# Two moves in the order of a transformer's layer slots: a norm's second parts behind the divisions, a residual between two steps of Q's rotation

## The chip, the cores and the metric

The kernel runs on one core of one Trainium2 chip. The metric is device time in microseconds (us) of one execution. The core has five engines that run beside each other and wait for one another through semaphores: TensorE (PE; its weight loads are listed apart as PEld), VectorE (DVE), ScalarE (ACT), GpSimd (POOL) and SyncE (SP), which issues the transfers. TensorE writes to PSUM, of which there are eight banks.

## The reference

Four sequences of 512 tokens with 128 channels pass through one attention of 16 heads and then through six layers. All is in float32. A layer is a local attention and a gated feed-forward step (FFN), each with a token shift ahead of it and a residual behind it:

```python
def attn_layer(x, Wqkv, qs, ksc, Wo):
    q, k, v = jnp.split(x @ Wqkv, 3, -1)      # 16 heads of 64
    q = l2norm(q) * qs
    k = l2norm(k) * ksc
    q = q * cos * scale + rotate_half(q) * sin * scale
    k = k * cos * inv + rotate_half(k) * sin * inv
    out = local_attention(q, k, v)            # windows of 32, each with the one before it
    return out @ Wo

def ffn_layer(x, g, bln, W1, b1, W2, b2):
    mu = x.mean(-1, keepdims=True)
    var = ((x - mu) ** 2).mean(-1, keepdims=True)
    xn = (x - mu) / jnp.sqrt(var + 1e-05) * g + bln
    a, gate = jnp.split(xn @ W1 + b1, 2, -1)
    return a * jax.nn.gelu(gate, approximate=False) @ W2 + b2

for i in range(DEPTH):                        # 6
    x = attn_layer(shift_tokens(x), ...) + x
    x = ffn_layer(shift_tokens(x), ...) + x
```

## The kernel before

The first 569 us or so hold the attention ahead of the layers, which the change does not touch. The layers are worked as a pipeline of 96 units: layer by layer, sequence by sequence, tile by tile of 128 tokens (four tiles, T = 0 to 3, to a sequence). A loop calls `slot(n, ...)` for n = -1 to 94, and each slot works on several units at once:

- unit n (`u`): its scores, softmax and product with V;
- unit n-1 (`prev`): its output projection and residual;
- unit n+1 (`nxt`): the transposes of its Q and K;
- unit n+2 (`new`): the projections of its Q, K and V, and the rotation of Q and K.

Between them stand, by a plan, the steps of the FFN of the sequence before. For a sequence whose FFN begins in the slot n of a first tile (T = 0), the shift of its tokens (`move`) stands in slot n, the norm's mean, variance and scale (`norm`) in slots n+1 to n+3, so in T = 1 to 3, and the FFN's chunks and its output (`geglu`) in slots n+3 to n+6. Each of the three norm steps has a second part: a Square on ScalarE (L104) behind the mean; the reciprocal root behind the variance (two VectorE steps, L81 and L82, and twelve GpSimd steps, L84 to L87); and one VectorE step with the norm's gain and bias (L123, tile hT) behind the scale. A second part is not issued at once but put into the list `later`.

The order of the work is written out by hand: each engine works its instructions in the order in which the kernel's scheduled program holds them. The lines that matter here, with the engine of each:

- L659 and L670 (PE): scores; L680 and L682 (DVE): their maximum and its subtraction; L688 (ACT): exponents.
- `project`, L521 (PE): a projection of 1024 columns in two halves of 512, into two PSUM banks. `square`, L533 (ACT), and `sum_squares`, L538 (DVE), give the norms of the heads.
- `rotate`, L543 and L549 (DVE): the two products of the rotation, both read from PSUM; between them it can issue other steps (`between`). `add_rotated`, L560 (POOL), adds the two. `over_norm`, L568 (POOL), divides by the norms; ahead of it come L564, L81 and L82 (DVE) and L84 to L87 (POOL).
- `transposed`, L632 (PE) and L635 (ACT): four transposes into one bank, and the copy out of it; for P (tile pr, copy pT), Q, K and the output. Two banks (`one_t`) serve these, the output projection and the norms.
- `times_v`, L702 (PE), in two groups; L711 and L712 (DVE): the division of each.
- `project_out_2`, L727 (PE), and `residual`, L735 (DVE), which reads the projection's bank.
- FFN: shift L153 to L155 (POOL); chunk L771 and L772 (PE), L775 (ACT), L779 (DVE); output L791 (PE), L794 (DVE).

In the slot of a first tile (`first`) the kernel before projects one half of K, rotates Q and issues the residual ahead of the transposes of P; the other half of K stands between the two groups of these transposes. In the other slots the residual comes first, K's first half stands between the transposes and its other half behind them, with Q's rotation. In all slots the list `later` is issued between the two products of K's rotation.

Of the kernel before, what the change touches and what calls it, by code (L numbers as in the profile page):

```python
# [32 lines left out]
def body(ctx: ExitStack, tc: tile.TileContext, a, out: bass.AP):  # L33
# [37 lines left out]
    def new_xT():  # L71
        return res.tile([P, S], F32, tag="xT", name="xT", bufs=B + 2)
# [102 lines left out]
    with tc.manual_schedule():  # L175
# [105 lines left out]
        class Rows:  # L281
# [5 lines left out]
            def scores(self):  # L287
                b, c, t = self.b, self.c, self.t
                sc = self.sc = ps1.tile([P, 2, S], F32, tag="sc", name="ps_sc", bufs=2)
                for k0 in range(0, S, S // 2):  # L290
                    for h in range(2):
                        rows = slice(h * HD, (h + 1) * HD)
                        mm(
                            sc[:, h, k0 : k0 + S // 2],
                            lhsT=qs[b, c][rows, t * P : (t + 1) * P],
                            rhs=ks[b, c][rows, k0 : k0 + S // 2],
                            start=(k0 == 0),
                            stop=False,
                            skip_group_check=True,
                        )  # L300
# [173 lines left out]
    def load_part(i, j):  # L474

        w = wts.tile([P, INNER], F32, tag=f"wqkv{j}", name=f"wqkv{j}_{i}")
        nc.sync.dma_start(out=w, in_=a["wqkv"][i, :, j * INNER : (j + 1) * INNER])
        return w
# [19 lines left out]
    def two_t(k, name):  # L498
        k = (part[0] + k) % 3
        return ps.tile([P, 2, 512], F32, tag=f"two{k}", name=name, bufs=1)  # L500

    def one_t():
        return ps_one.tile([P, 512], F32, tag="one", name="ps_one", bufs=2)

    def heads(ap):
        return ap.rearrange("p (h d) -> p h d", d=HD)
# [10 lines left out]
    def project(u, j, c0=0, c1=2):  # L517
        p = u.p[j] if c0 else two_t(((1, 2, 1), (0, 2, 1), (1, 2, 0))[min(u.n, 2)][j], "ps_proj")
        u.p[j] = p
        for c in range(c0, c1):  # L520
            mm(  # L521
                p[:, c, :],
                lhsT=u.xs[:, u.T * P : (u.T + 1) * P],
                rhs=wpart[j][:, c * 512 : (c + 1) * 512],
                start=True,
                stop=True,
            )
        if c1 == 2:
            u.p[j] = flat(p)

    def square(u, j):
        u.sq[j] = s2a.tile([P, INNER], F32, tag="t1", name="sq", bufs=4)
        nc.scalar.activation(u.sq[j], u.p[j], AF.Square)  # L533
# [6 lines left out]
    def rotate(u, j, between=()):  # L540
        t0 = u.r[j] = s2a.tile([P, INNER], F32, tag="rot", name="rot", bufs=6)
        lt, pf, half = u.lt, u.p[j], HD // 2
        nc.vector.tensor_tensor(  # L543
            heads(t0), heads(pf), lt[:, u.T, 2 * j].unsqueeze(1).to_broadcast([P, HEADS, HD]), ALU.mult
        )
        for f in between:
            f()
        t1 = u.t1 = s2a.tile([P, INNER], F32, tag="t1", name="t1", bufs=4)
        nc.vector.tensor_tensor(  # L549
            t1.rearrange("p (h t d) -> p h t d", t=2, d=half),  # L550
            pf.rearrange("p (h t d) -> p h t d", t=2, d=half)[:, :, ::-1, :],
            lt[:, u.T, 2 * j + 1]
            .rearrange("p (t d) -> p t d", t=2)
            .unsqueeze(1)
            .to_broadcast([P, HEADS, 2, half]),
            ALU.mult,
        )

    def add_rotated(u, j):
        nc.gpsimd.tensor_tensor(u.r[j], u.r[j], u.t1, ALU.add)  # L560
# [134 lines left out]
    def times_v(u, g):  # L695
        if g == 0:
            u.on = s2.tile([P, NC, 2, HD], F32, tag="on", name="on", bufs=1)
        o = two_t(g, "ps_att")
        for c in range(4):
            for j in range(NW):  # L700
                for h in range(2):
                    mm(  # L702
                        o[j * W : (j + 1) * W, h, c * (HD + 1) : (c + 1) * (HD + 1)],
                        lhsT=u.pT[h * HD : (h + 1) * HD, 4 * g + c, j * W : (j + 1) * W],
                        rhs=u.vw[h * HD : (h + 1) * HD, j, 4 * g + c, :],
                        start=True,
                        stop=True,
                    )
        ov = o[:, :, 0 : 4 * (HD + 1)].rearrange("p a (c d) -> p a c d", d=HD + 1)
        rden = small.tile([P, 2, 4, 1], F32, tag="rden", name="rden")  # L710
        nc.vector.reciprocal(rden, ov[:, :, :, HD : HD + 1])  # L711
        nc.vector.tensor_tensor(  # L712
            u.on[:, 4 * g : 4 * g + 4].rearrange("p c a d -> p a c d"),
            ov[:, :, :, 0:HD],
            rden.to_broadcast([P, 2, 4, HD]),
            ALU.mult,
        )
# [11 lines left out]
    def residual(u):  # L729
        if u.T == 0:  # L730
            u.xn = new_xT()
        else:
            u.xn = units[u.n - 1].xn
        cols = slice(u.T * P, (u.T + 1) * P)
        nc.vector.tensor_tensor(u.xn[:, cols], u.y[:, 0:P], xT[u.b][:, cols], ALU.add)  # L735
        if u.T + 1 == NT:
            xT[u.b] = u.xn
# [86 lines left out]
    def unit(n):  # L824
        return units[n] if 0 <= n < len(units) else None

    def follower(u):
        return units[u.n + 1] if u.T + 1 < NT else None

    def begin(u):  # L830

        if u is None or u.T:
            return
        if u.n == 0:
            xs, lt = start
        else:
            xs = shifted(u.b)
            lt = layer_tables(u.i) if u.b == 0 else units[u.n - 1].lt
        for v in units[u.n : u.n + NT]:
            v.xs, v.lt, v.p = xs, lt, [None] * 3  # L840

    def do_project(u, j, c0=0, c1=2):
        project(u, j, c0, c1)
        if c1 == 2 and u.b + 1 == B and u.T + 1 == NT and u.i + 1 < L:
            wpart[j] = load_part(u.i + 1, j)
# [25 lines left out]
    def slot(n, norm, move, geglu):  # L871

        u, prev, nxt, new = unit(n), unit(n - 1), unit(n + 1), unit(n + 2)
        part[0] = (-1 - n) % 3
        begin(unit(n + 4))
        if u:
            scores(u)  # L880
            exponents(u)
        if new:
            do_project(new, 0)
            square(new, 0)
        if n == -1:
            y = one_t()
            project_out1(B - 1, y)
        for f in norm:
            f()
        if prev:  # L890
            project_out_2(prev)
            if prev.b + 1 == B and prev.T + 1 == NT and prev.i + 1 < L:
                wo_w[0] = load_wo(prev.i + 1)


        first = u is not None and u.T == 0
        if prev and not first:
            residual(prev)
        if new and first:
            do_project(new, 1, 0, 1)  # L900
            rotate(new, 0)
            add_rotated(new, 0)
        if prev and first:
            residual(prev)
        for f in move:
            f()
        if u:
            transpose_p(u, 0)
        if new:
            do_project(new, 1, 1 if first else 0, 2 if first else 1)  # L910
        if u:
            transpose_p(u, 1)
        if new and not first:
            rotate(new, 0)
            add_rotated(new, 0)
            do_project(new, 1, 1)
        if new:
            square(new, 1)
        if n == -1:
            residual1(B - 1, y)  # L920
        if u:
            times_v(u, 0)
            times_v(u, 1)
        if new:
            sum_squares(new, 0)
            rotate(new, 1, later)
            later.clear()
            add_rotated(new, 1)
            sum_squares(new, 1)
        if nxt:  # L930
            transpose_q(nxt)
        if new:
            do_project(new, 2, 0, 2 if geglu else 1)
        if new and geglu:
            v_windows(new, follower(new))
        if nxt:
            transpose_k(nxt)
        if new and not geglu:
            do_project(new, 2, 1)
            v_windows(new, follower(new))  # L940
        if n == -1:
            third_step()
        if nxt:
            carry_k(nxt, follower(nxt))
        if new:
            inverse_norms(new)
            over_norm(new, 0)
            over_norm(new, 1)
        for f in geglu:
            f()  # L950
        if u:
            transpose_o(u)

    with tc.manual_schedule():
        begin(units[0])
        later = []
# [41 lines left out]
        u, prev = units[end - 1], units[end - 2]  # L998
# [144 lines left out]
```

## Time and profile before

| | |
|---|---|
| median of three runs | 2213.39 us (2212.27 to 2214.37) |
| profiled execution | 2211.16 us |
| its span, first to last instruction | 2209.3 us |
| PE busy | 2143.7 us, 97% |
| DVE busy | 1702.8 us, 77% |
| POOL busy | 1510.9 us, 68% |
| ACT busy | 1360.1 us, 62% |
| mean granted clock of TensorE | 0.994 |

A page of the profile gives, for one execution, each engine's busy time, groups of equal instructions by line with their mean duration, and the idle time ahead of them with what ended it. A line of the waits reads: engine, tile and line that waited, what it waited for, us in total, how often, the longest. A line of the timeline reads: start in us from the span's start, us taken, engine, line, operation, tiles written and read, shapes, count of merged instructions, and in brackets the idle time before it with what ended it. TensorE's matmuls are pipelined and their ends modelled, so starts are safer to compare than ends. Busy shares are means over the whole span; what a move is worth is read in its own slot.

### The profile page before, as it was taken

What the parts mean: (1) busy time and instruction counts of PE and PEld (TensorE: products, weight loads), DVE (VectorE), ACT (ScalarE), POOL (GpSimd) and SP (SyncE); (2) the same over time, 40 slices, a digit from 0 to 9 for tenths busy, and PEclk for the clock granted to TensorE, in tenths of its full rate; (3) what the DMA queues carried; (4) which work ended last, traced back from release to release, by engine and by line L of the source; (5) the groups of instructions that cost most, each with busy time, mean ns of one, the idle gap of its engine ahead of it and who ended that gap; (6) DMA issues with size and microseconds to landing.
All of it is one profiled execution on the core that took longest, in us unless ns stands there. A gap on an engine that the chain in (4) does not pass through costs nothing.

```text
span 2209.3 us, 82380 instructions
## 1 busy us (share of the span) xinstructions
PE 2143.7 (97%) x35150; PEld 1435.1 (65%) x35150; DVE 1702.8 (77%) x2501; ACT 1360.1 (62%) x2589; POOL 1510.9 (68%) x2281
## 2 busy tenths in 40 slices
PE   7999999999999999999999999999999999999997
PEld 5565656554666666666666666666666666666665
DVE  3676767666788788888888878888888788878884
ACT  3675656655456666665666666666666666666663
POOL 2554545554878787787777777777777777777772
PEclk8999999999999999999999999999999999999999
DMA  3000000000322233232332323223232223322230
GB/s 119 1 1 1 1 1 1 1 1 1 72 66 71 66 89 75 65 75 61 94 77 62 74 67 95 69 63 78 69 95 66 66 73 86 82 64 64 68 72 27
DMA packets 91063, 125.76 MB, mean 57 GB/s; under 512 B 25422, under 2 KB 39500, under 8 KB 90700
## 3 DMA queue, kind: packets, MB, share of 16 engines
q1 hardware_dynamic: 89996, 118.79, 21.8%
q8 instruction: 280, 4.59, 0.9%
q10 hardware_dynamic: 704, 1.70, 0.2%
q14 instruction: 83, 0.68, 0.1%
HBM read 20.31 MB, written 1.05 MB: 10 GB/s over the span
## 4 chain that ended last, share of the span: by engine, by line
PE 64%; DVE 9%; issue 1%; ACT 1%; POOL 0%; ACTq 0%; DVEq 0%; POOLq 0%
PE ps_proj L521 20%; PE ps_one L632 13%; PE ps_one L727 7%; PE ps_att L702 6%; PE ps_att L670 6%; PE ps_proj L771 3%; PE ps_proj L772 3%; PE ps_proj L791 3%; DVE ss L538 2%; DVE rot L543 2%; DVE on L712 2%; PE ps_att L659 1%; PE ps_one L109 1%; PE ps_one L100 1%; DVE t L549 1%
## 5 line engine op out<-in xcount | busy, mean ns | idle before, releaser
L521 PE MATMUL ps_proj<-wqkv,xs 128*128 128x512 f32 x1152 | 570.9, 603 | 1.8 <-issue 1.8
L560 POOL TENSOR_TENSOR rot<-rot,t 128x1024 f32<-128x1024 f32 x192 | 454.0, 2365 | 171.5 <-DVE t L549 147.5
L347 POOL TENSOR_TENSOR pr<-pr,den 128x1024 f32<-128x1024 f32 x128 | 241.1, 1894 | 248.3 <-DVE den L344 240.5
L568 POOL TENSOR_TENSOR rot<-rot,ss 128x1024 f32<-128x1024 f32 x192 | 362.1, 1907 | 7.5
L543 DVE TENSOR_TENSOR rot<-ps_proj,lt 128x1024 f32<-128x1024 f32 x192 | 233.9, 1218 | 60.3 <-ACT sq L533 60.0
L521 PEld LDWEIGHTS ps_proj<-wqkv,xs 128*128 128x128 f32 x1152 | 188.8, 191 | 103.9 <-issue 95.5
L688 ACT ACTIVATE pr<-pr 128x1024 f32<-128x1024 f32 x96 | 101.5, 1057 | 235.3 <-DVE pr L682 235.3
L549 DVE TENSOR_TENSOR t<-ps_proj,lt 128x1024 f32<-128x1024 f32 x192 | 233.3, 1215 | 0.0
L538 DVE TENSOR_REDUCE ss<-sq 128x16 f32<-128x1024 f32 x192 | 232.1, 1209 | 0.0
L333 ACT ACTIVATE pr<-ps_sc,nm 128x128 f32<-128x128 f32 (+3 forms) x448 | 220.6, 511 | 5.8 <-DVE nm L320 5.4
L533 ACT ACTIVATE sq<-ps_proj 128x1024 f32<-128x1024 f32 x192 | 195.2, 1017 | 41.3 <-PE ps_proj L521 38.9
L320 DVE TENSOR_REDUCE nm<-ps_sc 128x2 f32<-128x1024 f32 x128 | 156.0, 1219 | 82.8 <-PE ps_sc L308 82.8
L632 PEld LDWEIGHTS ps_one<-ident,rot 128*128 128x128 f32 x1536 | 172.9, 141 | 66.9 <-issue 56.0
L632 PE MATMUL ps_one<-ident,rot 128*128 128x128 f32 x1536 | 206.2, 277 | 5.8 <-issue 4.8
L727 PEld LDWEIGHTS ps_one<-aT,wo 128*128 128x128 f32 x1536 | 182.8, 192 | 24.4 <-issue 23.7
L727 PE MATMUL ps_one<-aT,wo 128*128 128x128 f32 x1536 | 189.2, 276 | 0.7 <-issue 0.4
L84 POOL TENSOR_TENSOR yt<-y 128x32 f32<-128x32 f32 (+2 forms) x384 | 88.8, 231 | 138.9 <-DVE y L82 95.3
L635 ACT COPY pT<-ps_one 128x512 f32<-128x512 f32 x192 | 112.5, 586 | 94.1 <-PE ps_one L632 93.7
L635 ACT COPY qT<-ps_one 128x512 f32<-128x512 f32 x192 | 103.4, 589 | 100.7 <-PE ps_one L632 100.7
L614 ACT COPY vt<-ps_proj 128x512 f32<-128x512 f32 x192 | 103.1, 589 | 96.6 <-PE ps_proj L521 96.6
L358 PEld LDWEIGHTS ps_pt<-ident,pr 128*128 128x128 f32 x1024 | 117.8, 142 | 56.9 <-issue 47.1
L680 DVE TENSOR_REDUCE mx<-ps_att 128x16 f32<-128x1024 f32 x96 | 117.2, 1221 | 48.1 <-PE ps_att L670 47.0
(173 smaller groups left out, 4101.3 us busy)
## 6 DMA issues: line engine op xcount, KB each, us to landing
vw<-vt SPq DMA_DIRECT2D x1152, 65.0 KB
vw_first<-vt SPq DMA_DIRECT2D x336, 65.0 KB
wqkv<-in_wqkv_dram SPq DMA_DIRECT2D x18, 512.0 KB
wo<-in_wo_dram SPq DMA_DIRECT2D x6, 512.0 KB
w<-in_w_dram SPq DMA_DIRECT2D x6, 341.0 KB
xr<-in_x_dram SPq DMA_DIRECT2D x3, 256.0 KB
scales<-in_scales_dram SPq DMA_DIRECT2D x6, 128.0 KB
w<-in_w_dram SPq DMA_DIRECT2D x12, 64.0 KB
```

The source lines that it names most:

```text
L333: nc.scalar.activation(self.pr[:, h, cols], self.sc[:, h, cols], AF.Exp, bias=self.nm[:, part_, h : h + 1], accum_out=self.den[:, part_, h ...
L347: nc.gpsimd.tensor_tensor(self.pr, self.pr, self.den[:, 0].unsqueeze(2).to_broadcast([P, 2, S]), ALU.mult)
L521: mm(p[:, c, :], lhsT=u.xs[:, u.T * P : (u.T + 1) * P], rhs=wpart[j][:, c * 512 : (c + 1) * 512], start=True, stop=True,)
L533: nc.scalar.activation(u.sq[j], u.p[j], AF.Square)
L538: nc.vector.tensor_reduce(u.ss[:, j * HEADS : (j + 1) * HEADS], heads(u.sq[j]), AX.X, ALU.add)
L543: nc.vector.tensor_tensor(heads(t0), heads(pf), lt[:, u.T, 2 * j].unsqueeze(1).to_broadcast([P, HEADS, HD]), ALU.mult)
L549: nc.vector.tensor_tensor(t1.rearrange("p (h t d) -> p h t d", t=2, d=half), pf.rearrange("p (h t d) -> p h t d", t=2, d=half)[:, :, ::-1, :],
L560: nc.gpsimd.tensor_tensor(u.r[j], u.r[j], u.t1, ALU.add)
L568: nc.gpsimd.tensor_tensor(heads(u.r[j]), heads(u.r[j]), u.ss[:, j * HEADS : (j + 1) * HEADS].unsqueeze(2).to_broadcast([P, HEADS, HD]), AL ...
L632: nc.tensor.transpose(tp[:, c * P : (c + 1) * P], src[:, (4 * g + c) * P : (4 * g + c + 1) * P], ident)
L635: nc.scalar.copy(dst[:, 4 * g : 4 * g + 4, col0 : col0 + P], tp.rearrange("p (c t) -> p c t", c=4))
L727: mm(y[:, 0:P], lhsT=wo_w[0][:, c, :], rhs=u.aT[:, c, :], start=(c == 0), stop=(c == NC - 1))
```

## The change

The list `later` is issued behind the two divisions of `times_v`, ahead of Q's sum of squares, no longer within K's rotation. In the slots of first tiles the residual is issued between the two products of Q's rotation instead of behind Q's rotation and its add, and the second half of K is projected behind both groups of P's transposes instead of between them. No instruction is added or removed.

```diff
             residual(prev)
         if new and first:
             do_project(new, 1, 0, 1)
-            rotate(new, 0)
+            rotate(new, 0, [lambda: residual(prev)] if prev else ())
             add_rotated(new, 0)
-        if prev and first:
+        elif prev and first:
             residual(prev)
         for f in move:
             f()
         if u:
             transpose_p(u, 0)
-        if new:
-            do_project(new, 1, 1 if first else 0, 2 if first else 1)
+        if new and not first:
+            do_project(new, 1, 0, 1)
         if u:
             transpose_p(u, 1)
         if new and not first:
             rotate(new, 0)
             add_rotated(new, 0)
+        if new:
             do_project(new, 1, 1)
-        if new:
             square(new, 1)
         if n == -1:
             residual1(B - 1, y)
         if u:
             times_v(u, 0)
             times_v(u, 1)
+        while later:
+            later.pop(0)()
         if new:
             sum_squares(new, 0)
-            rotate(new, 1, later)
-            later.clear()
+            rotate(new, 1)
             add_rotated(new, 1)
             sum_squares(new, 1)
```

## The prediction

> **What bounds the kernel now.** I read the page first, then the waits of TensorE, then the timelines, engine by engine, of four slots in a row (865 to 932 us). Of the page:
>
> ```profile
> PE 2143.7 (97%) x35150; PEld 1435.1 (65%) x35150; DVE 1702.8 (77%) x2501; ACT 1360.1 (62%) x2589; POOL 1510.9 (68%) x2281
> ...
> PEclk8999999999999999999999999999999999999999
> ```
>
> TensorE is at work 97% of the span at a granted clock that the page shows as 9 tenths or more in all slices but the first. The change removes no work, so all it can win is TensorE's idle time, and all it can lose is new idle time there. In the stretch 580 to 2160 us TensorE is busy 1550.7 of 1580.0 us: 29.3 us are idle. Of the waits:
>
> ```profile
> PE ps_att L702 <- issue: 9.3, 7, 1.9
> ...
> PE ps_proj L771 <- DVE hT L123: 5.8, 18, 0.8
> ...
> PEld ps_proj L771 <- DVE hT L123: 11.2, 21, 1.0
> ```
>
> The second and third are one stall: the first FFN chunk (L771) waits for the norm's last part (L123). I call the slots T0 to T3 by the tile T of their unit; a cycle of four takes 67.0 us here (865.2 to 932.2 us). L123 runs in T3:
>
> ```profile
> 895.24 1.04 PE L632 MATMUL ps_one<-ident,rot 128*128 128x128 f32 x8
> 896.58 1.13 PE L771 MATMUL ps_proj<-hT,w 128*128 128x512 f32 x2 [0.31 <-DVE hT L123]
> ...
> 893.13 0.69 DVE L712 TENSOR_TENSOR on<-ps_att,rden 128x512 f32<-128x512 f32 x1
> 893.74 1.21 DVE L538 TENSOR_REDUCE ss<-sq 128x16 f32<-128x1024 f32 x1
> 894.86 1.22 DVE L543 TENSOR_TENSOR rot<-ps_proj,lt 128x1024 f32<-128x1024 f32 x1
> 895.99 0.54 DVE L123 TENSOR_SCALAR hT<-hT,vecs 128x512 f32<-128x512 f32 x1
> ```
>
> K's transposes begin at 895.24 and L771 at 896.58, 1.34 us later; in the next slot (T0), where nothing is awaited, the same two begin at 911.96 and 912.83, 0.87 apart. The stall is 0.47 us. The second place is the middle of T0 (slot start 899.37):
>
> ```profile
> 904.83 1.02 PE L521 MATMUL ps_proj<-wqkv,xs 128*128 128x512 f32 x2
> 905.69 0.60 PE L632 MATMUL ps_one<-ident,pr 128*128 128x128 f32 x4
> 906.12 1.02 PE L521 MATMUL ps_proj<-wqkv,xs 128*128 128x512 f32 x2
> 906.98 0.63 PE L632 MATMUL ps_one<-ident,pr 128*128 128x128 f32 x4
> 907.55 1.83 PE L702 MATMUL ps_att<-vw_first,pT 64*32 64x65 f32 x128
> 909.31 1.09 PE L632 MATMUL ps_one<-ident,rot 128*128 128x128 f32 x8
> ...
> 906.32 0.59 ACT L635 COPY pT<-ps_one 128x512 f32<-128x512 f32 x1 [0.33 <-PE ps_one L632]
> ...
> 907.17 1.21 DVE L549 TENSOR_TENSOR t<-ps_proj,lt 128x1024 f32<-128x1024 f32 x1
> ```
>
> The order on TensorE is half of K, first P transposes, other half of K, second P transposes, P times V. The second transposes start 0.07 us after the first pT copy's end (906.91), and the weight loads' row there names that copy as releaser. So they use the bank that the first ones used, and the other half of K stands exactly in the time of that copy.
>
> **Part 1: the norm's second parts before the sum of squares.** 22 norms. No instruction is added. In T1 the part is a Square on ScalarE; in the built order ScalarE's queue is unchanged, so nothing. In T2 it is L81 and L82 (0.16 and 0.17 us) with twelve small steps on GpSimd; in T3 it is L123.
>
> T3: L123 would start at about 893.74 instead of 895.99, so hT is ready near 894.3, and L771 needs it at 896.11. The stall goes whole. Measured this way in each T3 slot it is 0.28 to 0.47 us in twenty, 0.95 in the first and nothing in the last: 9.6 us, between the bounds 5.8 and 11.2 of the two rows. VectorE's own chain is not shorter: L538, L543 and L549 follow L123 now, and L549 ends at 897.66 as before.
>
> T2: GpSimd's twelve steps stood from 879.46 to 882.76, and held back the add of K's rotation behind them (L560, 882.71, while its input was ready at 880.51). Begun 2.25 us earlier they end at 880.5, and L560 runs 880.7 to 883.05. This has a price and a gift, both read from two rows of L564, VectorE's first step behind the sums: 0.18 us where no L560 ran beside it (T2) and 1.39 us in T3, ending at 900.21, 0.04 after L560's end. In T2 it will now be held to 883.1, and L794 behind it ends 1.25 us after L560 (as L779 does in T3), at 884.3 instead of 882.93. Next on VectorE is the maximum of T3's scores at 884.65, which waits for TensorE: 0.3 us of cover, cost nothing. The gift: GpSimd enters T3 1.3 us earlier, so its add of Q's rotation, 892.64 to 895.00 now, is bound by its input (L549 of Q, end 891.53, plus 0.18) and ends near 894.05. L123 at 893.74 meets only its tail: I take 0.05 us. If GpSimd did not come earlier, L123 would be held to about 895.3, 1.0 us more; the one L123 that did overlap an L560 took 1.36 us.
>
> [...]
>
> **Part 2: T0.** The order and the waits in which the changed kernel is built show for all 24 first tiles: half of K, both P transposes, other half of K, P times V; and in 23 of them the second transposes still wait for the first pT copy. (The one without a preceding unit waits for another step.) The residual's earlier place does not give them the bank of the output projection. So the second transposes stay at 906.98, and from 906.12 to 906.98 TensorE has nothing: 0.86 us, the issue time of half of K. From there: other half of K at +0.48 (four transposes take 0.43 when streaming, 905.69 to 906.12, and 0.57 from a wait to L702), L702 at +0.95 (923.48 to 924.43 in T1), Q's transposes at +1.44 (891.15 to 892.59 in T3): 909.85 instead of 909.31. Loss 0.54, not 0.86, because the old L702 held a stall: its second half waits for L549 (end 908.38, 908.50 on the load row), and now comes later than that. With each slot's own times: 0.50 to 0.58 in eighteen, 0.66 to 0.72 in four where L549 was not late, 0.18 in one, 0 in one: 12.6 us.
>
> The residual (0.28 us, 0.20 from start to next start) now stands ahead of L549. Behind L549 wait L702's second half and GpSimd's L560. GpSimd is busy till 909.94 with other steps, so nothing there; the FFN's shift on GpSimd, which needs the residual, stands behind that L560 and gains nothing either. For L702 see next.
>
> **What is late next.** Part 1 brings T0's start 0.47 us forward, but not VectorE: L779, which ends at 901.42 after L564, now sets the maximum (901.51), and so exponents (end 905.08), Q's square (906.00), the pT copy and L549, at 0.1 earlier at most. The copy can start at about 905.85; by TensorE (0.47 earlier) also at 905.86. Both ends meet: the gain just fits. In the six or so slots whose transposes came earlier than in this one, it does not, 0.05 to 0.17 each, 0.6 in all. L549 would end at 908.49 and release L702's half at 908.61; TensorE comes to it at 908.68. With margins of 0.01 and 0.07 any delay of VectorE costs: I take 1.6 us (0.6, and 1.0 for L123's tail in 22 slots), between 0.6 (no tail) and 2.6 (a tail of 0.09).
>
> **Sum.** +12.6 + 1.6 − 9.6 = +4.6 us. The profiled execution is 2211.16 us (span 2209.3, 1.9 around it), so 2215.8; the median of the three runs stands 2.2 above it, and I carry that: 2218.0, +0.21%.
>
> **Rivals.**
> 1. *Not slower: TensorE's irregular waits.* Of the 29.3 idle us, 23.5 are not L123's; the rows show waits of up to 1.9 us for nothing visible ("issue", 7 times at L702). They fall in different slots, so they may depend on when the queue stands where. If more than 9.0 of them went, the kernel would be 0.2% faster; with half gone, 2206. For it: slots of one kind differ by 1 to 2 us. Against: the three runs lie within 2.1 us, so they repeat, and the instruction counts stay.
> 2. *Slower: L123 collides with GpSimd's add.* Place: T3, 893.74. It decides if GpSimd's add ends after 894.2. At the full 1.0 us, exponents and copy in T0 come 1.0 later, 22 times: 2218 + 21 = 2239; a third of it, 2225. Against: the 2.25 us of head start in T2.
> 3. *No difference.* T0's loss is that of the copy alone and T0's margins hold: 12.6 − 9.6 and a little luck, 2213 to 2216.
>
> **How the numbers follow.** I count 0.2% (4.4 us) as what a measurement can tell from no change: 2209.0 to 2217.8. As worked: 0.66, its own range 2214 to 2222, of which 0.38 lies above 2217.8 and 0.28 within. Rival 1: 0.14 (0.12 faster, 0.02 within). Rival 2: 0.12, slower. Rival 3: 0.08, within. Faster 0.12, within 0.38, slower 0.50. The range 2209 to 2225 leaves out most of rival 1 and half of rival 2, near 0.18.
>
> **What would show it.** After: no wait of L771 for L123; in T0 the two P transposes next to each other with about 0.86 us idle between, released by ScalarE's pT copy; Q's transposes 5.0 us behind the start of K's first half, where it is 4.5 now (904.83 to 909.31); T3 slots 16.2 instead of 16.7 us, T0 slots 16.5 to 16.7 instead of 16.0 to 16.2; L564 in T2 at 1.4 instead of 0.18 us; L123 at 0.55 to 0.6. I am wrong if the second transposes start without that copy's end (faster by 8), or if L123 takes over 0.9 us (slower).

## The result and the profile after

The changed kernel takes 2221.77 us (median of six runs, 2218.65 to 2225.29); the kernel before, run beside it, 2212.43 us (2208.13 to 2214.37). The ratio is 1.0039, with a 95% interval of 1.0022 to 1.0055: slower by 9.3 us. The profiled execution of the changed kernel is its median run, 2221.77 us with a span of 2220.0 us; that of the kernel before has 2209.3 us, so the two traces differ by 10.7 us. A second set of runs of the same kernel (below) gives 1.0040 (1.0026 to 1.0054).

The prediction was 2218.0 us, in a range of 2209 to 2225: the side and the range held, but of the difference it gave only half, 4.6 us where 9.3 were measured. The page's first line and the waits of TensorE, after (engine, tile, line, what it waited for: us, times, longest):

```profile
PE 2143.0 (97%) x35150; PEld 1434.7 (65%) x35150; DVE 1726.5 (78%) x2501; ACT 1360.4 (61%) x2589; POOL 1514.1 (68%) x2281
```

```profile
PE ps_one L632 <- ACT pT L635: 16.3, 23, 0.7
PE ps_att L702 <- issue: 10.1, 9, 1.8
...
PE ps_att L670 <- issue: 5.0, 8, 1.3
PE ps_one L632 <- issue: 4.9, 5, 2.6
```

Both rows of L771 waiting for L123 are gone. At the top stands a new wait, of P's second transposes for the first pT copy, 23 times. The irregular "issue" waits are there as before, and somewhat longer. VectorE is busy 23.7 us more: the same instructions, some of them now beside GpSimd's (L564 takes 129.0 us in all where it took 104.4, L123 14.4 where it took 13.2).

T3, the slot that held the stall (timeline of after; the slot starts at 889.31):

```profile
901.90 1.04 PE L632 MATMUL ps_one<-ident,rot 128*128 128x128 f32 x8
902.77 1.02 PE L771 MATMUL ps_proj<-hT,w 128*128 128x512 f32 x2
...
899.77 0.69 DVE L712 TENSOR_TENSOR on<-ps_att,rden 128x512 f32<-128x512 f32 x1
900.38 0.61 DVE L123 TENSOR_SCALAR hT<-hT,vecs 128x512 f32<-128x512 f32 x1
900.90 1.21 DVE L538 TENSOR_REDUCE ss<-sq 128x16 f32<-128x1024 f32 x1
...
898.33 2.36 POOL L560 TENSOR_TENSOR rot<-rot,t 128x1024 f32<-128x1024 f32 x1 [0.57 <-DVE t L549]
```

L771 follows K's transposes after 0.87 us (1.34 before) and waits for nothing. L123 stands behind the second division and takes 0.61 us instead of 0.54: GpSimd's add (L560) ends at 900.69, so the two run together for 0.3 us.

The end of the T2 slot ahead of it, where VectorE and GpSimd now meet:

```profile
888.29 1.31 DVE L564 TENSOR_SCALAR ss<-ss 128x32 f32<-128x32 f32 x1
...
887.21 2.35 POOL L560 TENSOR_TENSOR rot<-rot,t 128x1024 f32<-128x1024 f32 x1
```

Before, this L564 had no L560 beside it:

```profile
881.66 0.18 DVE L564 TENSOR_SCALAR ss<-ss 128x32 f32<-128x32 f32 x1
```

It now takes 1.31 us where it took 0.18, and ends 0.04 us after L560. T0, the slot behind that T3 (start 905.46):

```profile
910.82 1.02 PE L521 MATMUL ps_proj<-wqkv,xs 128*128 128x512 f32 x2
911.68 0.64 PE L632 MATMUL ps_one<-ident,pr 128*128 128x128 f32 x4
913.05 0.66 PE L632 MATMUL ps_one<-ident,pr 128*128 128x128 f32 x4 [0.73 <-ACT pT L635]
913.54 1.02 PE L521 MATMUL ps_proj<-wqkv,xs 128*128 128x512 f32 x2
914.50 1.61 PE L702 MATMUL ps_att<-vw_first,pT 64*32 64x65 f32 x128
916.04 1.09 PE L632 MATMUL ps_one<-ident,rot 128*128 128x128 f32 x8
...
912.42 0.58 ACT L635 COPY pT<-ps_one 128x512 f32<-128x512 f32 x1
...
907.39 0.75 DVE L779 SCALAR_TENSOR_TENSOR tmp_t<-ps_proj,vecs,tmp_t 128x512 f32<-128x512 f32 x1
908.05 1.22 DVE L680 TENSOR_REDUCE mx<-ps_att 128x16 f32<-128x1024 f32 x1
...
913.90 1.22 DVE L549 TENSOR_TENSOR t<-ps_proj,lt 128x1024 f32<-128x1024 f32 x1
```

The two groups of P's transposes stand next to each other, the second 0.05 us behind the copy's end (913.00), with TensorE idle between. Q's transposes begin 5.22 us behind K's first half (4.48 before). VectorE's gated product L779 (end 908.14) runs straight into the maximum L680, 0.8 us behind the end of TensorE's scores (907.28). Before, scores and L779 ended within 0.13 us of each other (901.29 and 901.42):

```profile
900.67 0.75 DVE L779 SCALAR_TENSOR_TENSOR tmp_t<-ps_proj,vecs,tmp_t 128x512 f32<-128x512 f32 x1
901.51 1.23 DVE L680 TENSOR_REDUCE mx<-ps_att 128x16 f32<-128x1024 f32 x1
```

I timed each slot from its first score (L659) to the next slot's, and took the 21 slots of each kind between slot 8 and slot 91 of the two traces, and what lies around them:

| part of the span | before, us | after, us | difference |
|---|---|---|---|
| 21 slots T0 (median of one) | 339.8 (16.10) | 356.2 (16.80) | +16.4 |
| 21 slots T1 | 357.3 (16.69) | 359.5 (16.74) | +2.3 |
| 21 slots T2 | 371.5 (17.56) | 370.1 (17.50) | −1.4 |
| 21 slots T3 | 355.1 (16.69) | 344.3 (16.15) | −10.9 |
| ahead of the first slot | 568.9 | 569.4 | +0.5 |
| slots 0 to 7 | 127.3 | 128.4 | +1.1 |
| slots 92 to 94, and the rest | 89.5 | 92.1 | +2.7 |
| sum | 2209.3 | 2220.0 | +10.7 |

T0 and T3 hold the change: +5.5 us, where the prediction had +4.6. The "issue" waits fall into these slots too: with them taken off slot by slot, T0 and T3 together are 3.4 us longer here, and 4.9 in the profile of the second set. The other 5 us lie where the change moves next to nothing.

### The profile page after: what moved, and what is told of

It reads as the page before. It is cut to its first block, busy times and chain, and to the rows that moved or that the text cites. A ratio compares the mean times of both kernels' runs of the same rounds, so it can differ in the third digit from the quotient of the medians.

```text
span 2220.0 us, 82380 instructions
## 1 busy us (share of the span) xinstructions
PE 2143.0 (97%) x35150; PEld 1434.7 (65%) x35150; DVE 1726.5 (78%) x2501; ACT 1360.4 (61%) x2589; POOL 1514.1 (68%) x2281
## 3 DMA queue, kind: packets, MB, share of 16 engines
q1 hardware_dynamic: 89996, 118.79, 21.7%
## 4 chain that ended last, share of the span: by engine, by line
PE 59%; DVE 12%; issue 2%; ACT 2%; POOL 1%; SPq 0%; DMA 0%; DVEq 0%; ACTq 0%; POOLq 0%
PE ps_proj L521 18%; PE ps_one L632 13%; PE ps_one L727 6%; PE ps_att L702 6%; PE ps_att L670 5%; PE ps_proj L791 3%; DVE ss L538 2%; PE ps_proj L771 2%; PE ps_proj L772 2%; DVE ss L564 1%; DVE on L712 1%; DVE rot L543 1%; DVE t L549 1%; DVE pr L682 1%; PE ps_att L659 1%
## 5 line engine op out<-in xcount | busy, mean ns | idle before, releaser
L560 POOL TENSOR_TENSOR rot<-rot,t 128x1024 f32<-128x1024 f32 x192 | 454.3, 2366 | 211.9 <-DVE t L549 191.1
L549 DVE TENSOR_TENSOR t<-ps_proj,lt 128x1024 f32<-128x1024 f32 x192 | 232.9, 1213 | 0.0
L632 PEld LDWEIGHTS ps_one<-ident,pr 128*128 128x128 f32 x768 | 90.4, 141 | 80.5 <-issue 39.8
```

What stands on the lines that cost most here:

```text
L549: nc.vector.tensor_tensor(t1.rearrange("p (h t d) -> p h t d", t=2, d=half), pf.rearrange("p (h t d) -> p h t d", t=2, d=half)[:, :, ::-1, :],
L632: nc.tensor.transpose(tp[:, c * P : (c + 1) * P], src[:, (4 * g + c) * P : (4 * g + c + 1) * P], ident)
```

## The experiments

The theory at that point: the change is a gain in T3, a larger loss in T0 by the bank that the P transposes share, and a scatter that comes from elsewhere. The change has three parts: besides the two of the title, K's second half moves behind both of P's transposes. The runs come in three groups, each beside its own runs of the kernel before; the median of that one was 2215.5 us in the first group, 2216.5 in the second and 2215.1 in the third. Each ratio below is against the kernel before.

### Each part alone

**The second parts behind the divisions, alone.**

```diff
+        while later:
+            later.pop(0)()
         if new:
             sum_squares(new, 0)
-            rotate(new, 1, later)
-            later.clear()
+            rotate(new, 1)
```

> Only the list of second parts is issued behind the divisions; the first tiles' slots stay as before. Theory A (in a first tile's slot VectorE's chain sets when Q's rotation ends, whatever TensorE does): the T3 slots fall from 16.7 to 16.1 us, L771 no longer waits for L123, but in T0 the second half of L702 is still released by L549 at the old time, so the T0 slots grow from 16.1 to about 16.6; in all 0 to 3 us faster (2209 to 2213). Rival B (the stall's whole time is won, because TensorE is the bound everywhere): T0 stays at 16.1 us and the time falls by about 10 us, to 2202.

Measured 2211.98 us, ratio 0.9977 (0.9967 to 0.9987): 5.1 us faster by the ratio. T3 takes 16.17 us, nearly as after; T0 takes 16.61 instead of 16.10, and a new row stands among the waits:

```profile
PE ps_att L702 <- DVE t L549: 10.1, 21, 0.6
```

So the 0.51 us won in T3 is all but given back in T0, with P's transposes still in their old place: there the second half of P times V comes 0.5 us too early for L549. The rival, that the gain stays, is refuted. Of the 4.3 us between the two profiled spans, the 84 slots hold 1.8, and 3.8 lie ahead of the first slot, where nothing was edited. TensorE's granted clock differs there (below, with the irregular waits); so by the profiles the edit itself is worth nearer 2 than 5.

**K's second half behind both transposes, alone.**

```diff
         if u:
             transpose_p(u, 0)
-        if new:
-            do_project(new, 1, 1 if first else 0, 2 if first else 1)
+        if new and not first:
+            do_project(new, 1, 0, 1)
```

(and the second half behind them, as in the change)

> Only the second half of K is projected behind both groups of P's transposes; residual and second parts stay as before. Theory A (the second transposes wait for the first pT copy because both groups use one bank, and nothing else fills that time): TensorE idles about 0.7 us visibly (0.86 from start to start) ahead of the second transposes in each T0 slot, the old stall on L549 goes, T0 slots 16.1 to 16.65 us; in all 11 to 14 us slower (2223 to 2227). Rival B (the gap is made up later in the slot): under 4 us slower.

Measured 2230.42 us, ratio 1.0054 (1.0039 to 1.0069): +12 us. T0 takes 16.68 us, 0.58 more, and the waits show both stalls side by side:

```profile
PE ps_one L632 <- ACT pT L635: 15.5, 23, 0.7
...
PE ps_proj L771 <- DVE hT L123: 5.6, 18, 0.8
```

L702 begins 0.86 us later in T0, by the issue time of the half of K that no longer covers the copy, and its own stall gives 0.33 of that back (from its first half to Q's transposes it takes 1.44 us here, 1.77 before). The slots lose 0.58 times 22 or 23, about 13. This is the term of 12.6.

**The residual between the products of Q's rotation, alone.**

```diff
-            rotate(new, 0)
+            rotate(new, 0, [lambda: residual(prev)] if prev else ())
             add_rotated(new, 0)
-        if prev and first:
+        elif prev and first:
             residual(prev)
```

> Only the residual is issued between the two products of Q's rotation in first tiles. Theory A: L549 ends 0.20 us later, and as L702's second half waits for it in most T0 slots, these grow by 0.2 us: 4 to 5 us slower (2216 to 2218). Rival B (the residual's place is of no account, since nobody waits for it): within 1 us of before.

Measured 2228.59 us, ratio 1.0048 (1.0034 to 1.0062): +10.6 us, about twice what was expected. The mechanism is there: L549 ends at 9.19 us into T0 instead of 8.96, and L702's second half begins 0.23 later; the median T0 is 16.36, so 0.26 times 23, 6 us. The rest is not this stall:

```profile
PE ps_att L702 <- issue: 18.7, 13, 2.4
```

9.3 us stood in this row before. Nothing in the edit touches L702's own waits for nothing visible; what they are is asked below. The two longest of them, in slots 52 and 80, are each followed by 3.4 us at half of TensorE's granted clock, where the kernel before has none.

### What sets T0 after the change

**The change, with the residual ahead of Q's rotation.**

```diff
-        if prev and not first:
+        if prev:
             residual(prev)
...
-            rotate(new, 0, [lambda: residual(prev)] if prev else ())
+            rotate(new, 0)
...
-        elif prev and first:
-            residual(prev)
```

> The changed kernel with the residual ahead of Q's rotation, where VectorE waits for Q's square anyway; by the built order the second P transposes then use the bank of the output projection and wait for the residual, no longer for the first pT copy. Theory A: no idle time of TensorE ahead of the second transposes; the next wait is L702's second half for L549, about 9.6 us into the slot; T0 slots 16.5 us instead of 16.8; 5 to 8 us faster than the changed kernel (2214 to 2217 beside 2221.8). Rival B (the copy's wait is not what costs): as the changed kernel, 2220 to 2224.

Measured 2214.95 us, ratio 0.9999 (0.9985 to 1.0013). With the residual ahead, the projection's bank is free for the second transposes, so they no longer wait for the copy; T0 takes 16.61 us, the value of the second parts alone. L549 ends at 9.46 us into the slot and L702's second half begins at 9.60: it waits for VectorE again (the profile puts the wait down to L711, the short step that follows L549 there):

```profile
PE ps_att L702 <- DVE rden L711: 9.5, 19, 0.7
```

So the bank costs about 0.2 us a slot here and VectorE's chain the other 0.5.

**The second parts and the residual ahead, K's second half between the transposes.**

```diff
-        if prev and not first:
+        if prev:
             residual(prev)
...
+        while later:
+            later.pop(0)()
```

> Edit: the kernel before with the list of second parts behind the divisions, and in a first tile the residual ahead of K's first half; K's second half stays between the transposes of P. Theory A (VectorE's gated product L779, not TensorE, sets first tiles once the stall on L123 is gone): the residual on VectorE leaves the middle of the slot, but the chain from L779 over maximum, exponents and L549 to the second half of P times V stays where it is; first tiles take 16.5 to 16.6 us, third-place tiles 16.1, and the time is 3 to 6 us below the kernel before, as with the second parts alone (ratio 0.997 to 0.9985). Theory B (the residual ahead of L549 was what held first tiles): first tiles go back to 16.1 us, and the time is 10 to 12 us below (ratio 0.995).

Measured 2217.44 us, ratio 1.0006 (0.9995 to 1.0018). The slots are those of theory A: T0 16.61, T3 16.13, L549's end at 9.45. The time is not: it lies some 5 us above what was expected. The residual is not what holds L549; the chain ahead of it is. Where the 5 us went is not shown.

**The gated product behind the next slot's softmax.** L779 is issued behind L682 of the next slot, for all three chunks:

```diff
+        while gates:
+            gates.pop(0)()
...
+        def chunk(f, k):
+            gates.append(f.chunk(k, 1, True))
...
-                plan(geglu, n + 3 + k, at(f.chunk, k, 1))
+                plan(geglu, n + 3 + k, at(chunk, f, k))
```

with the second parts behind the divisions.

> Edit: the kernel before with the list of second parts behind the divisions, and the FFN chunk's gated product (L779) issued in the following slot behind the steps of its softmax instead of at the end of its own slot. Theory A (L779 ahead of the maximum is what gives the gain back in first tiles): the maximum starts when the scores are there, first tiles return to about 16.05 to 16.1 us with last tiles at 16.13, so some 0.5 us in each of 22 cycles: 10 to 12 us below the kernel before (ratio 0.995), less or more by 2 to 3 us of TensorE's irregular waits. Theory B (the gain is given back by the irregular waits, whatever VectorE's order): first tiles stay at 16.6 us and the time is within 3 us of that with the second parts alone (ratio 0.997 to 0.9985). If the gate comes too late for the FFN's output (L791), a new wait of TensorE for L779 appears and the kernel is slower than with the second parts alone.

Measured 2216.44 us, ratio 0.9998 (0.9985 to 1.0011). T0 went back to 16.07 us with T3 at 16.15: theory A's slots. A cycle of four slots is 0.54 us shorter by its medians, 12 us in 22 cycles, and the time is the same as before. The waits say where the 12 us went:

```profile
PE ps_att L702 <- issue: 18.5, 12, 2.4
...
PE ps_proj L791 <- DVE tmp_t L779: 2.4, 1, 2.4
```

The last FFN's output waits 2.4 us for its own gated product, which comes too late there, and TensorE's granted clock stands at half for 6.8 us from that wait on: the six matmuls of L791 take 5.49 us where they take 2.82 in the kernel before. So slots 92 to 94 lost 5.3 us. And the "issue" waits of the layers sum to 30.3 us instead of 17.2.

**The same with the residual ahead.** Both edits together.

> Edit: both of the two edits above together: second parts behind the divisions, residual ahead of K's first half in a first tile, and the chunk's gated product behind the next slot's softmax. Theory A (L779 alone holds first tiles): the same time as with the gated product moved and the residual in its old place, 10 to 12 us below the kernel before (ratio 0.995). Theory B (L549 behind the residual holds the second half of P times V as well): another 0.2 us in each of 22 cycles, 14 to 16 us below (ratio 0.993).

Measured 2213.72 us, ratio 0.9993 (0.9982 to 1.0004); T0 16.07, T3 16.14, "issue" waits 24.2 us. The residual's place adds nothing once L779 is away; neither theory's time was reached, for the same reasons (L791 waits 2.2 us here, and 6.8 us at half clock follow).

### TensorE's irregular waits

I numbered all records of TensorE in the trace in order (matmuls, weight loads and sequencer steps: 71754). In the kernel before, all 20 "issue" waits over 0.15 us behind the first unit end at a number that is 193 to 195 modulo 256. The page's table of DMA queues (packets, MB, share) has a queue that fits:

```profile
q8 instruction: 280, 4.59, 0.9%
```

280 packets of 16384 bytes for 71754 records are one for 256. I paired them in order, each packet with a block of 256 records, the blocks parted at the number 193 modulo 256 and the first packet put to the block from record 449 on; one block sooner, most packets would start behind their block's beginning (median 1.0 us). So counted, a packet starts 2.3 us or more ahead of the first instruction of its block (the shortest of 254; median 5.9), and at the 20 waits it is 2.3 to 2.9 us: the waits are where TensorE arrives that early. (Of the other 234 blocks, 8 begin within 3.0 us too, without a wait over 0.15 us.) Scores or P times V run through 256 records in 1.5 to 1.8 us.

At 234 of the 254 boundaries between blocks behind the first unit no such wait stands; the other 20 cost 17.2 us here, up to 30.3 in the runs above.

**The kernel before, with 64 small products in front.**

```diff
+        p = bank1()
+        for _ in range(64):
+            mm(p[0:W, 0:W], lhsT=ident16[0:HD, 0:W], rhs=ident16[0:HD, 0:W], start=True, stop=True)
         make_q(0, 0)()
```

> Edit: the kernel before with 64 small matmuls of 32x32 (128 TensorE instructions with their weight loads) put in near the start, and nothing else; their results are not used. Theory A (the waits of TensorE that the profile ends by nothing come at every multiple of 256 of its own instructions, when the next packet of the instruction queue is awaited): the waits stay at a count of 193 to 195 modulo 256 but fall on other instructions of the slots, half a block away; the slots hit are others, the longest waits move, and the time differs from the kernel before by up to 5 us either way beside the matmuls' own 2 to 5 us. Theory B (they belong to the work: certain lines or slots): they stay at the same slots and lines, and their count modulo 256 moves by 128; the time is that of the kernel before plus 2 to 5 us.

Measured 2220.09 us, ratio 1.0016 (1.0003 to 1.0030). The first slot comes 2.0 us later; TensorE also has 6.8 us more at half clock ahead of it, so the 2.0 are not shown to be the products' own. There are 21 "issue" waits of 21.7 us in all, and every one ends at 193 or 194 modulo 256 again, but in other slots: those over 1.1 us fell in slots 13, 21, 27, 49, 85 and 94 before, now in 6, 17, 20, 23, 45 and 76 (2.9 us there). No regular slot changed (medians within 0.07 us). They belong to the count, not to the work.

**The changed kernel once more.** No edit.

> Edit: none; the changed kernel once more, beside the kernel before and the three kernels below on one chip, because both scatter by several us from run to run. Theory A (the regular loss is 0.2 us in a cycle of four slots, some 5 us, and the rest is TensorE's irregular waits, which differ from run to run): 4 to 10 us above the kernel before, slots of first tiles 16.8 us and of last tiles 16.1 us in its profile, as in the first run. Theory B (the first difference of 9 us was the chip's): within 3 us of the kernel before.

Measured 2224.80 us, ratio 1.0040 (1.0026 to 1.0054), T0 16.80 and T3 16.15 us. So the 9 us are the kernel's, and not those of one chip's runs. "Issue" waits: 20.0 us in the first profile and 22.6 in this one, against 17.2.

**A second scatter: the granted clock.** The profile also tells which clock TensorE was granted. It is full, but for stretches at half, of 3.4 us or a multiple (in the kernel before 13.7, 6.8 and 3.4 us) and one of 3.9 to 4.0 at the span's end; how many there are differs between profiles in code that no edit touched. Ahead of the first slot the kernel before spends 20.5 us at half clock and the second parts alone 13.7 (the stretch from 538.3 to 545.2 us is missing there); their first slots come at 568.9 and 565.0 us. Over all fourteen profiles this sum goes from 13.7 to 27.3 us and the first slot from 564.7 to 570.8, nearly in step (correlation 0.97). In the layers, every such stretch but the one at each span's end begins during a TensorE wait of 1.5 us or more or within 2.5 us of its end. Not every such wait brings one: the longest of the changed kernel, 2.6 us at 799 us, brought none. No run changed the clock by itself, so that the waits cause the stretches is likely, not shown.

### A version that beats both

**Only the first chunk's gated product behind the softmax**, with the second parts behind the divisions:

```diff
+        def chunk(f, k):
+            g = f.chunk(k, 1, True)
+            gates.append(g) if k == 0 else g()
...
```

> Edit: second parts behind the divisions, and of the FFN's three gated products (L779) only the first, which is the one ahead of the first tile's maximum, behind the next slot's softmax. Theory A (that one alone holds first tiles): first tiles 16.05 to 16.1 us and last tiles 16.13 as with all three moved, without the 2.4 us wait of the last FFN's output and the 5 us that the last four slots lost with all three moved: 3 to 5 us below that kernel, 0.997 to 0.9985 of the kernel before, if TensorE's irregular waits stay near 25 us; if they fall back to the 17 us of the kernel before, 0.994. Theory B (the three belong together): first tiles at 16.3 us or more.

Measured 2207.15 us, ratio 0.9972 (0.9960 to 0.9984). T0 16.08, T3 16.15, no wait of the FFN's output. VectorE's queue in T0 of this kernel (timeline):

```profile
899.94 0.18 DVE L82 TENSOR_SCALAR y<-yt 128x32 int32<-128x32 int32 x1
900.18 1.23 DVE L680 TENSOR_REDUCE mx<-ps_att 128x16 f32<-128x1024 f32 x1
901.44 1.23 DVE L682 TENSOR_TENSOR pr<-ps_att,mx 128x1024 f32<-128x1024 f32 x1
902.58 0.74 DVE L779 SCALAR_TENSOR_TENSOR tmp_t<-ps_proj,vecs,tmp_t 128x512 f32<-128x512 f32 x1
```

The maximum follows L82 directly, at 2.07 us into the slot instead of 2.59 after the change, and L779 fills time in which VectorE waits for ScalarE's exponents anyway. So L779 ahead of the maximum is what gave T3's gain back. The slots show this; the time does not: the ratio is hardly below that of the second parts alone (0.9977, intervals overlapping), though T0 is 0.52 us shorter in each cycle, some 11 us. Of these, the profiles show 3.6 us in more "issue" waits, and besides these 4.1 ahead of the first slot and behind slot 94, where this kernel has more time at half clock (6.8 and 2.3 us more).

**The same with the residual ahead of K's first half.**

> Edit: the same with the residual of a first tile ahead of K's first half as well. Theory A (VectorE has slack in first tiles once the gated product is away): the same as without the residual's move, within 3 us. Theory B (the residual ahead of L549 still holds the second half of P times V): 3 to 5 us faster than without it.

Measured 2209.57 us, ratio 0.9973 (0.9962 to 0.9984), T0 16.08 us: no difference, theory A.

**The same, with 16 small products behind the first warm-up** (64 TensorE instructions where TensorE waits for the first input):

```diff
         warm(10)
+        p = bank1()
+        for _ in range(16):
+            mm(p[0:W, 0:W], lhsT=avg[:, 0:W], rhs=avg[:, 0:W], start=True, stop=True)
         load_x(0)
```

> Edit: the kernel just above, with 16 small products of 32 columns (64 TensorE instructions) right behind the first warm-up products, where TensorE waits 3.3 us for the first input anyway. Theory A (irregular waits come at every multiple of 256 TensorE instructions and cost most where the boundary falls behind a burst): no slot's regular time changes, the waits stay at a count of 193 to 195 modulo 256, their sum changes by several us either way and the time with it, by up to 8 us. Theory B (where the boundary falls does not matter): the same sum of irregular waits within 3 us, and the same time.

Measured 2207.27 us, ratio 0.9962 (0.9949 to 0.9976). All 24 "issue" waits are at 193 to 195 modulo 256, in other slots than without the shift, and sum to 20.4 us instead of 21.3 (T0 and T2 keep their medians within 0.04 us; T3's is 16.27, 0.14 more): the boundaries moved, as theory A has it, but their cost in all did not, as theory B has it, and the two ratios' intervals overlap. It is the fastest ratio measured, 8.4 us below the kernel before, but not shown to be faster than the two kernels above it.

## Why the prediction was right, and where it was too small

**T3's stall goes whole: right, and a little more.** Predicted 0.47 us in a typical slot and 9.6 us in all; the median slot is 0.54 shorter, the 21 slots 10.9 us. What is on top stands in L771 itself: from its start to L772's it took 0.96 us when it began from a wait and takes 0.86 now. The prediction's own lines had this (1.13 us from the wait, 1.02 for an equal group that streams), and its sum left it out.

**L123 beside GpSimd's add: right.** Its median went from 0.54 to 0.605 us, 0.06 each where 0.05 was taken; GpSimd came early enough, as worked out from T2. L564 in T2 was predicted at 1.4 and took 1.31. With GpSimd's add at its old times, L123 would by the estimate of the prediction's second rival have cost 21 us more; with the new times it costs about 1 (L123 takes 14.4 us in all where it took 13.2), the prediction's 1.0 for its tail in 22 slots.

**T0, the copy in the open: right in its mechanism, under-sized by 0.16 us a slot.** Predicted 0.54 (16.5 to 16.7 us with VectorE's part), measured 0.70. P's second transposes and K's second half lie where they were put: medians over 21 slots give 7.61 us into the slot for the second transposes (7.60 before) and 9.06 for L702 (8.16). The term that failed is the length of L702, 0.10 of the 0.16. The prediction let it fall from 1.76 to 1.44 us, taking its stall on L549 as gone, with a margin of 0.07. It fell to 1.54: L549 now ends at 9.66 us into the slot (8.96 before), and L702's second half begins at 9.81 where 9.72 would do. The margin went the way the prediction feared: T3 brought T0's start 0.54 forward and not 0.47, TensorE came earlier and VectorE, held by L779, did not. The 1.6 us for "both ends meet" were too few by about 2.

**The sum for T0 and T3: +5.5 where +4.6 stood.** Larger gain, larger loss: the two misses mostly cancel. That the sum is so near is in part luck: without the "issue" waits in these slots it is 3.4 us, and 4.9 in the second profile.

**The irregular waits: the term set to nothing.** They were carried at no change, with a rival only for their shrinking, and the reason given was that the instruction counts stay. The counts do stay, and so do the boundaries; what changes is what TensorE does when it comes to one. "Issue" waits grew by 2.8 us in the first profile and by 5.4 in the second. In the fourteen profiles of this study their sum lies between 16.9 and 30.3 us, and the kernel before, with 17.2, stands at the low end: a reordering of it had more to lose there than to win. That was to be seen from the prediction's own numbers only in part, but a price of 0 to +5 belonged in the sum.

**The granted clock: not in the prediction.** Behind slot 94 the changed kernel took 1.8 us more in the first profile and 0.3 in the second. The first has a stretch of 3.4 us at half clock there, from 2194.1 us, that neither the second nor the kernel before has; at half clock, where the six matmuls of L791 took 5.49 us instead of 2.82, 3.4 us hold by my estimate some 1.7 us of TensorE's work. T0 and T3 without "issue" waits give 3.4 us of the first profile's 10.7, all these waits 2.8, and what follows slot 94, without its one such wait, 1.4. The other 3.1 lie scattered over the rest of the span and stay open.

**Rivals.** That the irregular waits shrink: they grew. That L123 collides with the add: 0.06 us, not 1.0. No difference: refuted by both sets of runs. What the prediction named as proof that it is wrong (the transposes without the copy, L123 over 0.9 us) did not come.

## What to carry to other kernels

When a stall on the bound engine is removed, look at once for the chain that does not move with it: here VectorE's product L779 stood ahead of the next slot's maximum, and a gain of 0.54 us in one slot was a loss of 0.5 in the next until that product was moved into time in which VectorE waits. Where two groups of instructions share a bank, look at the work that stands between them: here half of K covered the wait for the copy, and taking it away cost its length, less what a later stall gave back (0.86 less 0.33 us). With a scatter that is tied to an instruction count, price every reordering with the spread over several kernels, not with the value of the one profile that you have. And before you read a difference out of two profiles, compare the granted clock in the parts that no edit touched.

## What the runs showed of the hardware

Behind the first unit, TensorE's waits of over 0.15 us without a visible releaser come only where the number of its own records passes a fixed place modulo 256 (193 to 195), in all fourteen profiles, and at 19 to 27 of some 254 such places. With packets and blocks paired in order, a block's packet starts 18 to 298 records ahead of its first use in the kernel before and 0 to 301 after the change, and the soonest use is 2.2 to 2.3 us after that start. Why a packet starts late in one block and early in another stays open: its delay showed no relation to how many packets of V's transfers were under way (correlation −0.01 in the kernel before). VectorE's L564, on 128x32 numbers, took 0.18 us in the kernel before in the 22 cases with no add of GpSimd's (L560) beside it, and a median of 1.39 in the 74 with one, ending 0.04 us after it. TensorE's granted clock fell to half for 3.4 us or a multiple during or shortly behind some of its waits of 1.5 us or more, and the six matmuls of L791 took 5.49 us in such a stretch, 2.82 outside.
